# Eleven identity products during the first load, and the rests of the first group's odd heads moved together, in a decoder layer on one core

## The chip, the cores and the metric

The kernel runs on one core of a Trainium2 chip. A core has five engines that run beside each other and meet at semaphores: TensorE (PE in the profile; its weight loads are shown as PEld), VectorE (DVE), ScalarE (ACT), GpSimd (POOL) and SyncE (SP), which here only issues transfers. ACT and POOL issue a few transfers too. All transfers run on the core's 16 DMA engines. The metric is the device time of one execution in microseconds (us), the median of several.

## What is computed

One decoder layer over 16 sequences of 128 tokens with 256 channels, all in float32. It has three residual steps; only the first matters here, latent attention with 16 heads of 72 latent channels:

```python
h = layernorm(x)                                        # 16 x 128 x 256
Wdkv = h @ latent_w + latent_b                          # keys and values, 72 wide
q = einsum('btc,hcl->bhtl', h, Wd_w) + Wd_b[None, :, None, :]
scores = einsum('bhtl,bsl->bhts', q, Wdkv) / sqrt(16)   # then causal mask
y = einsum('bhts,bsl->bhtl', softmax(scores), Wdkv)
x = x + y.transpose(0, 2, 1, 3).reshape(b, t, 16 * 72) @ out_w + out_b
```

The second step mixes a context tensor in by a decaying sum that runs in both directions over the tokens (a WKV step). The third is a mixture of 8 experts of which each token uses two: tokens are sorted into lists by expert, and the experts' products run over slots of 128 listed tokens.

## The kernel before

**Stages.** Sequences are handled two at a time, a group (GB = 2, eight groups). A unit is one sequence with one set of four heads (HG = 4), so there are 64 units. A loop at the end of the program runs over steps: step s makes the scores, maxima and exponentials of unit s, normalizes unit s - 1, and turns the probabilities and makes the values of unit s - 2. The work of the next group, of the WKV step and of the routing is spread over the same steps by a written plan (`at(step, place, function)`; the places of a step are called "pre", A, B, C and D). After 64 steps come the expert slots. Each engine carries out its instructions in exactly the order in which the program writes them.

**The start.** Before the loop comes group 0's preparation, in this order: `masks()` makes two constants on POOL, identb (a 128 x 128 identity in bf16) and maskb (the causal mask of four heads, 128 x 512 in bf16). `group_stats(0)` and `group_norm(0)` normalize the first two sequences, `group_turn(0)` turns them on PE (L349) and `group_turned(0)` copies the result, xnT, out of PSUM on DVE (L353). `group_latents(0)` makes keys and values (L363), and `query_tile` (L404) with `query_tile_out` (L410, on ACT) makes and evicts query tiles 0 to 3. A float32 product shows in the trace as two instructions of half its work each, called halves below.

**Query tiles and rests.** Queries are made channels by tokens. Two heads of 72 channels would need 144 rows, but a tile has 128. So each of eight tiles (NP = 8) holds an even head's 72 channels and 56 of the odd head's (LB = 56); the 16 channels left over from each odd head (LR = 16) are made together in a ninth tile, `qrest`, the tile of the rests. Its weights `wqr_sb` are gathered by a POOL copy (L1206). Tiles 0 to 3 form the even set q0 (q[0, 0]), tiles 4 to 7 the even set q2 (q[0, 2]).

The odd sets q1 and q3 hold odd heads with all 72 channels in order. `odd_queries(g, u)` puts set 2u + 1 together by transfers from SBUF to SBUF: one copy of 56 partitions with 4 KB each from the even set (L422), and the 16 remaining rows. For group 0 the rests come from `qrest` by four transfers of 16 KB, one for each head (L425); later groups take another way by DRAM (L428).

**Order around the change.** `first_rest`, planned for step 0 at "pre", stands just behind the scores of unit 0. It makes and evicts the tile of rests, puts q1 together, and starts `load_outw()`: three transfers of 1152 KB in all, the weights of the output projection (L191 to L193), that are needed in step 5. Tiles 4 and 5 come in step 0, tiles 6 and 7 in step 1, and `odd_queries(0, 1)` puts q3 together in step 1 as soon as tile 7 is evicted. The scores of unit 1 (L440, L442) need q1, those of unit 2 need q2, those of unit 3 need q3. All these transfers are issued by SP, one after another; an issue that waits keeps all later ones back. ACT makes the exponentials of unit 1 ahead of the evictions of tiles 6 and 7.

**Pools.** `bank("mm", ...)` hands out PSUM banks from a pair in turn; latents and query tiles use it. Sets of queries live in `qpool`, with five buffers for tag "q", handed out in the order in which the program asks.

The functions that the change touches, with the lines that the profile names:

Of the kernel before, what the change touches and what calls it, by code (L numbers as in the profile page):

```python
# [9 lines left out]
F32 = mybir.dt.float32  # L10
# [8 lines left out]
P = 128  # L19
# [6 lines left out]
L = 72  # L26
# [5 lines left out]
GT = GB * T  # L32
HG = 4
# [3 lines left out]
NP = H // 2  # L37
LB = P - L
# [41 lines left out]
def decoder_kernel(  # L80
# [19 lines left out]
    nc = tc.nc  # L100
# [14 lines left out]
    qpool = st.enter_context(tc.tile_pool(name="qpool", bufs=5))  # L115
# [12 lines left out]
    def bank(tag, name, bufs=2):  # L128
        return psum.tile([P, 512], F32, tag=tag, name=name, bufs=bufs)
# [59 lines left out]
    def load_outw():  # L189
        outw2 = outw.rearrange("l (i o) c -> l i o c", o=2)  # L190
        nc.sync.dma_start(outw_sb[0:L, 0:NP, :], outw2[:, :, 0, :])  # L191
        nc.sync.dma_start(outw_sb[L:P, 0:NP, :], outw2[0:LB, :, 1, :])
        nc.sync.dma_start(  # L193
            outw_sb[:, NP, :], outw[LB:L].rearrange("r (i o) c -> (r i) o c", o=2)[:, 1, :]
        )
# [19 lines left out]
    identb = wpool.tile([P, P], BF16, tag="identb", name="identb")  # L215
    maskb = wpool.tile([P, HG, T], BF16, tag="maskb", name="maskb")
# [3 lines left out]
    def masks():  # L220
        nc.gpsimd.tensor_copy(identb, ident)
        nc.gpsimd.memset(maskb, 0.0)
        nc.gpsimd.affine_select(
            out=maskb,
            in_=maskb,
            compare_op=ALU.is_ge,
            fill=NEG,
            base=0,
            pattern=[[0, HG], [-1, T]],
            channel_multiplier=1,  # L230
        )
# [64 lines left out]
    def rstd_of(var, n, name):  # L296

        nc.vector.tensor_scalar_add(var, var, EPS)
        rs = small.tile([P, GB], F32, tag="rs", name=f"rs_{name}")
        nc.gpsimd.tensor_tensor(rs[:, :n], var, mhalf[:, :n], ALU.pow)  # L300
        return rs

    def stats(mv, src, name):
        bn = small.tile([P, 6], F32, tag="bn", name=f"bn_{name}")
        nc.vector.bn_stats(bn, src)
        nc.vector.bn_aggr(mv, bn)


    mva, rsa, xns, pxns, xnT, kvT, kvN, q, qrest = {}, {}, {}, {}, {}, {}, {}, {}, {}

    def group_stats(g):
        mva[g] = small.tile([P, GB, 2], F32, tag="mv4", name=f"mv4_{g}", bufs=2)
        for i in range(GB):
            stats(mva[g][:, i, :], xs[g * GB + i], f"a{g}_{i}")
        rsa[g] = rstd_of(mva[g][:, :, 1], GB, f"a{g}")
# [7 lines left out]
    def group_norm(g):  # L323
        mv, rs = mva.pop(g), rsa.pop(g)
        xns[g] = []
        nb = less_mean(mv[:, :, 0], rs, GB, f"a{g}") if g else None
        for i in range(GB):
            xt = xs[g * GB + i]
            xn = wk.tile([P, C], F32, tag="xn", name=f"xn_{g}_{i}")
            if g:  # L330
                nc.scalar.activation(
                    xn, xt, AF.Identity, bias=nb[:, i : i + 1], scale=rs[:, i : i + 1]
                )
            else:
                nc.vector.tensor_scalar(
                    xn, xt, mv[:, i, 0:1], rs[:, i : i + 1], ALU.subtract, ALU.mult
                )
            xns[g].append(xn)
# [51 lines left out]
    def query_tile(g, i):  # L390

        u, j = divmod(i, HG)
        if i == NP:
            qrest[g] = qpool.tile([P, GT], F32, tag="qr", name=f"qr_{g}", bufs=1)
            to = qrest[g]
            w = wqr_sb.rearrange("p c r i -> p c (r i)")
        else:
            if j == 0:
                q[g, 2 * u] = qpool.tile([P, HG, GT], F32, tag="q", name=f"q_{g}_{2 * u}")
            to = q[g, 2 * u][:, j, :]  # L400
            w = wq_sb[:, :, i, 0:P]
        pq = bank("mm", f"pq_{g}_{i}")
        for c in range(NC):
            nc.tensor.matmul(  # L404
                pq[:, :GT], w[:, c, :], xnT[g][:, c, :], start=(c == 0), stop=(c == NC - 1)
            )
        return pq, to

    def query_tile_out(g, i, pq, to):
        nc.scalar.activation(to, pq[:, :GT], AF.Identity, bias=bq_sb[:, i : i + 1], scale=0.25)  # L410
# [7 lines left out]

    def odd_queries(g, u):

        qb = qpool.tile([L, HG, GT], F32, tag="q", name=f"q_{g}_{2 * u + 1}")
        nc.sync.dma_start(qb[0:LB], q[g, 2 * u][L:P])  # L422
        if g == 0:
            for j in range(HG):
                nc.sync.dma_start(qb[LB:L, j, :], qrest[g][u * HG + j : P : NP, :])  # L425
        else:
            qd = qds[g].rearrange("(r i) t -> r i t", i=NP)
            nc.sync.dma_start(qb[LB:L], qd[:, ts(u, HG), :])  # L428
        q[g, 2 * u + 1] = qb


    pss, probs, sums_of, pts, aTs, pys, yP, yds, pos = {}, {}, {}, {}, {}, {}, {}, {}, {}
# [758 lines left out]


    masks()
    group_stats(0)
    group_norm(0)
    group_turn(0)
# [12 lines left out]

    def first_rest():  # L1210
        query_tile_out(0, NP, *query_tile(0, NP))
        odd_queries(0, 0)
        load_outw()

    at(0, "pre", first_rest)

    late_tiles = {0: [4, 5], 1: [6, 7]}
# [12 lines left out]
    for s in range(SLOT0 + len(ORDER) + 1):  # L1230
        j = s - SLOT0
# [22 lines left out]
        g, i = divmod(s, UG)  # L1254
# [12 lines left out]
        for n, t in tiles:  # L1267
            if t == NP:
                rest_queries(n)
            if t == 5 and n:  # L1270
                odd_queries(n, 0)
            if t == 7:
                odd_queries(n, 1)
# [68 lines left out]
```

## Time and profile before

| | |
|---|---|
| Three timed runs | 552.07, 553.12 and 553.45 us, median 553.12 |
| The profiled execution | 554.7 us; its span, from first to last instruction, 553.0 |
| Mean granted TensorE clock | 0.984 |
| First tokens' statistics on DVE begin | 3.68 us (they waited for the transfer of x) |
| First turn of group 0 on PE | 6.54 us |
| Scores of unit 0, unit 1, unit 2, unit 3 begin on PE | 15.64, 20.02, 24.37, 31.10 us |
| PE waited longest in total for | DVE xn (L349), 6.5 us, once, at the start |

The profile's times are microseconds from the start of the span. The timeline lists an engine's instructions in order; neighbours of one kind are merged and counted (x8 is eight of them). A PE line's length includes the modelled end of a pipelined product, so the pace is better read from the distance between starts. "Idle before <- releaser" gives how long the engine did nothing and what ended it. SPq and ACTq lines are issues of transfers: their length is that of the issue, not of the transfer. The windows view adds up each engine's busy time in a stretch, with the clock that TensorE was granted (1.00 is full) and the busy share of the DMA engines.

### The profile page before, as it was taken

Reading aid. Unit: us, or ns where it says so; the run is one execution under the profiler, and the core shown is the slowest. Engines: PE = TensorE matmul, PEld = TensorE weight load, DVE = VectorE, ACT = ScalarE, POOL = GpSimd, SP = SyncE. Lnnn points to the kernel's source line nnn. Section 1 sums busy time; section 2 is a strip of 40 time slices with the busy share of each in tenths; the row PEclk is TensorE's granted clock in tenths of the full one; section 3 lists DMA queues with packets and bytes.
Section 4 is the critical chain, followed back from the end, with each engine's and each line's share of the span. In section 5 each row is a group of like instructions: output and inputs, shape, how many; then the busy total and the mean of one; then the engine's idle time right before and its main releaser. Section 6 shows DMA issues by size and latency. Waiting matters only on the chain. (4 is left out here: it accounts for less than half of the span.)

```text
span 553.0 us, 10138 instructions
## 1 busy us (share of the span) xinstructions
PE 512.8 (93%) x3272; PEld 439.2 (79%) x3272; DVE 330.6 (60%) x831; ACT 329.3 (60%) x953; POOL 327.1 (59%) x379
## 2 busy tenths in 40 slices
PE   4889999999999999999998989999989999989990
PEld 3768787887777887877875679989979999989980
DVE  3354776687887678888769776555644533333330
ACT  1788998898797888888986873434313232313200
POOL 5356647564787774697646976454875454541532
PEclk9999999999999999999998999999989999999996
DMA  5432245364365545131121113232234232325321
GB/s 149 98 88 67 70 133 170 121 198 120 110 182 133 170 130 178 41 98 37 52 79 56 40 53 66 38 65 45 40 40 51 48 51 47 51 47 173 58 30 19
DMA packets 39662, 47.59 MB, mean 86 GB/s; under 512 B 14136, under 2 KB 31416, under 8 KB 39576
## 3 DMA queue, kind: packets, MB, share of 16 engines
q1 hardware_dynamic: 30106, 37.20, 23.0%
q0 software_dynamic: 7936, 9.51, 11.2%
q8 instruction: 28, 0.46, 0.3%
q10 hardware_dynamic: 1566, 0.21, 0.3%
q14 instruction: 26, 0.21, 0.2%
HBM read 28.22 MB, written 13.31 MB: 75 GB/s over the span
## 5 line engine op out<-in xcount | busy, mean ns | idle before, releaser
L467 ACT ACTIVATE pr<-s,nm 128x128 f32<-128x128 f32 x256 | 90.7, 370 | 9.7 <-DVE nm L459 9.5
L480 POOL TENSOR_TENSOR pr<-pr,rsum 128x512 f32<-128x512 f32 x64 | 75.7, 1183 | 33.5 <-DVE rsum L479 25.6
L990 ACT ACTIVATE sl<-s 128x512 f32<-128x512 f32 x36 | 21.5, 598 | 120.7 <-PE s L980 104.9
L1018 POOL DMA_INDIRECT acc<-y,en x28 | 47.5, 1697 | 60.4 <-DVE y L1013 29.8
L442 PEld LDWEIGHTS s<-kvT,q 72*128 72x128 f32 x512 | 65.7, 191 | 18.7 <-issue 12.6
L980 PEld LDWEIGHTS s<-xT,w 128*128 128x128 f32 x576 | 70.5, 195 | 9.4 <-issue 6.7
L980 PE MATMUL s<-xT,w 128*128 128x128 f32 x576 | 72.0, 279 | 5.4 <-DVE xT L944 2.3
L520 PE MATMUL po<-outw_sb,yP 128*128 128x256 f32 x288 | 74.4, 385 | 0.6 <-DMA yP<-yd 0.6
L442 PE MATMUL s<-kvT,q 72*128 72x128 f32 x512 | 70.5, 279 | 3.2 <-DMA q<-qr 2.2
L980 PE MATMUL pu<-xT,w 128*128 128x128 f32 x576 | 70.5, 276 | 0.0
L992 DVE TENSOR_TENSOR hT<-sl,pu 128x512 f32<-128x512 f32 x36 | 24.7, 687 | 74.1 <-PE pu L980 56.9
L1002 PE MATMUL pd<-wall,hT 128*128 x288 | 68.0, 379 | 0.0
L494 PE MATMUL py<-aT,kvN 128*72 128x512 f32 x128 | 66.4, 600 | 1.6 <-ACT aT L488 1.3
L980 PEld LDWEIGHTS pu<-xT,w 128*128 128x128 f32 x576 | 67.7, 193 | 0.0
L404 PE MATMUL pq<-xnT,wq_sb 128*128 128x256 f32 x256 | 65.3, 387 | 0.0
L520 PEld LDWEIGHTS po<-outw_sb,yP 128*128 128x128 f32 x288 | 54.0, 193 | 13.1 <-issue 5.2
L459 DVE TENSOR_REDUCE nm<-s 128x4 f32<-128x512 f32 x64 | 43.6, 682 | 30.5 <-PE s L442 30.5
L1002 PEld LDWEIGHTS pd<-wall,hT 128*128 128x128 f32 x288 | 52.0, 190 | 5.6
L467 ACT ACTIVATION_READ_ACCUMULATOR pr<-s,nm 128x1 f32 x256 | 53.0, 207 | 0.0
L488 ACT COPY aT<-pt 128x512 f32<-128x512 f32 x64 | 37.2, 581 | 26.0 <-PE pt L486 24.6
L404 PEld LDWEIGHTS pq<-xnT,wq_sb 128*128 128x128 f32 x256 | 46.2, 195 | 5.0 <-issue 0.2
L912 POOL DMA_INDIRECT xr<-xn,en x36 | 37.4, 1040 | 13.3 <-issue 7.6
(172 smaller groups left out, 877.8 us busy)
## 6 DMA issues: line engine op xcount, KB each, us to landing
wall<-in_wg_dram SPq DMA_DIRECT2D x8, 512.0 KB
wall<-in_wu_dram SPq DMA_DIRECT2D x8, 512.0 KB
wall<-in_wd_dram SPq DMA_DIRECT2D x8, 512.0 KB
q<-q SPq DMA_DIRECT2D x16, 224.0 KB
yP<-yB SPq DMA_DIRECT2D x32, 112.0 KB
cx<-in_cx_dram SPq DMA_DIRECT2D x16, 128.0 KB
acc<-x SPq DMA_DIRECT2D x16, 128.0 KB
xn<-row SPq DMA_DIRECT2D x16, 128.0 KB
```

Source lines behind the costliest of these rows:

```text
L404: nc.tensor.matmul(pq[:, :GT], w[:, c, :], xnT[g][:, c, :], start=(c == 0), stop=(c == NC - 1))
L442: nc.tensor.matmul(ps[:, j, :], q[g, hg][0:L, j, ts(i, T)], kvT[g][:, ts(i, T)], start=False, stop=(j == HG - 1), skip_group_check=n >= 2,)
L459: nc.vector.tensor_reduce(nm, ps, AX.X, ALU.max, negate=True)
L467: nc.scalar.activation(pr[:, j, :], ps[:, j, :], AF.Exp, bias=nm[:, j : j + 1], accum_out=sums[:, j : j + 1],)
L480: nc.gpsimd.tensor_mul(pr, pr, rsum.unsqueeze(2).to_broadcast([P, HG, T]))
L488: nc.scalar.copy(aT, pt)
L494: nc.tensor.matmul(py[:L], kvN[g][:, ts(i, L)], aTs.pop((b, hg)), start=True, stop=True)
L520: nc.tensor.matmul(pos[b][:, :C], yP[b][:, i, :], outw_sb[:, i, :], start=(i == 0), stop=(i == NP))
L912: nc.gpsimd.indirect_dma_start(out=xr, out_offset=None, in_=xn2[0 : t["rows"], :], in_offset=bass.IndirectOffsetOnAxis(ap=entries[j][:, 0: ...
L980: nc.tensor.matmul(o[:, ts(f, P)], w[:, c * F + f * P : c * F + (f + 1) * P], xT[:, c, :], start=(c == 0), stop=(c == NC - 1),)
L1002: nc.tensor.matmul(pd[:, :C], hT[:, f, :], wall[:, bass.ds(e, 1), WD0 + f * C : WD0 + (f + 1) * C], start=(f == 0), stop=(f == NF - 1),)
L1018: nc.gpsimd.indirect_dma_start(out=acc if j < SF + S2 else out2, out_offset=bass.IndirectOffsetOnAxis(ap=en[:, 1:2], axis=0), in_=y, in_of ...
```

## The change

Two things are changed. Behind `masks()`, eleven products of identb and maskb are written to a PSUM bank from the pair "mm" that nothing reads. And the rests of both odd sets are moved by a new function, `first_odd(u)`, that asks for the odd set's buffer and issues its four transfers from `qrest`. `first_rest` calls it for q1 ahead of `odd_queries(0, 0)`, and for q3 behind it; `odd_queries` of group 0 now only issues the copy of 56 partitions.

```diff
     def odd_queries(g, u):
 
-        qb = qpool.tile([L, HG, GT], F32, tag="q", name=f"q_{g}_{2 * u + 1}")
-        nc.sync.dma_start(qb[0:LB], q[g, 2 * u][L:P])
         if g == 0:
-            for j in range(HG):
-                nc.sync.dma_start(qb[LB:L, j, :], qrest[g][u * HG + j : P : NP, :])
+            qb = q[g, 2 * u + 1]
+            nc.sync.dma_start(qb[0:LB], q[g, 2 * u][L:P])
         else:
+            qb = qpool.tile([L, HG, GT], F32, tag="q", name=f"q_{g}_{2 * u + 1}")
+            nc.sync.dma_start(qb[0:LB], q[g, 2 * u][L:P])
             qd = qds[g].rearrange("(r i) t -> r i t", i=NP)
             nc.sync.dma_start(qb[LB:L], qd[:, ts(u, HG), :])
         q[g, 2 * u + 1] = qb
+
+    def first_odd(u):
+
+        q[0, 2 * u + 1] = qpool.tile([L, HG, GT], F32, tag="q", name=f"q_0_{2 * u + 1}")
+        for j in range(HG):
+            nc.sync.dma_start(q[0, 2 * u + 1][LB:L, j, :], qrest[0][u * HG + j : P : NP, :])
...
     masks()
+
+    idle = bank("mm", "idle")
+    for _ in range(11):
+        nc.tensor.matmul(idle, identb, maskb, start=True, stop=True)
     group_stats(0)
...
     def first_rest():
         query_tile_out(0, NP, *query_tile(0, NP))
+        first_odd(0)
         odd_queries(0, 0)
+        first_odd(1)
         load_outw()
```

On SP the order of issues from the tile of rests on becomes: before, copy q0 to q1, four rests of q1, three of outw, copy q2 to q3, four rests of q3; after, four rests of q1, copy q0 to q1, four rests of q3, three of outw, copy q2 to q3. The buffer of q3 is now asked for ahead of q2's. The products have line 1203 in the changed kernel, the rests line 435, the copies of group 0 line 423.

## The prediction

> **What bounds the kernel now.** I read the page first, its busy shares and slices, to see which engine carries the span.
>
> ```profile
> PE 512.8 (93%) x3272; PEld 439.2 (79%) x3272; DVE 330.6 (60%) x831; ACT 329.3 (60%) x953; POOL 327.1 (59%) x379
> ...
> PE   4889999999999999999998989999989999989990
> ```
>
> TensorE is the bound, except in the first three slices (13.8 us each), and the change lies wholly in those. So I read the timeline there.
>
> ```profile
> 2.29 0.64 POOL L223 TENSOR_SCALAR_AFFINE_SELECT maskb<-maskb 128x512 bf16<-128x512 bf16 x1
> ...
> 6.54 1.11 PE L349 MATMUL pxn<-ident,xn 128*128 128x128 f32 x4 [6.54 <-DVE xn L335]
> ...
> 8.44 1.98 PE L363 MATMUL pk<-xnT,latw_sb 128*72 128x256 f32 x4 [0.79 <-DVE xnT L353]
> ...
> 13.77 0.47 ACT L410 ACTIVATE q<-pq,bq_sb 128x256 f32<-128x256 f32 x1 [1.12 <-PE pq L404]
> 14.63 0.47 ACT L410 ACTIVATE q<-pq,bq_sb 128x256 f32<-128x256 f32 x1 [0.39 <-PE pq L404]
> ...
> 15.99 0.94 SPq L422 DMA_DIRECT2D q<-q  x1
> ...
> 17.60 0.47 ACT L410 ACTIVATE qr<-pq,bq_sb 128x256 f32<-128x256 f32 x1 [1.63 <-PE pq L404]
> ...
> 18.10 2.49 SPq L425 DMA_DIRECT2D q<-qr  x4
> ...
> 19.12 0.38 PE L440 MATMUL s<-maskb,identb 128*128 128x512 bf16 x1
> ...
> 19.99 0.30 PEld L442 LDWEIGHTS s<-kvT,q 72*128 72x128 f32 x2 [0.98 <-DMA q<-q]
> ...
> 20.63 0.91 SPq L191 DMA_DIRECT2D outw_sb<-in_outw_dram  x1
> 20.65 0.30 PEld L442 LDWEIGHTS s<-kvT,q 72*128 72x128 f32 x2 [0.36 <-DMA q<-qr]
> ...
> 22.20 1.89 PE L404 MATMUL pq<-xnT,wq_sb 128*128 128x256 f32 x8
> ...
> 26.05 0.82 SPq L422 DMA_DIRECT2D q<-q  x1
> ...
> 26.92 2.56 SPq L425 DMA_DIRECT2D q<-qr  x4
> ...
> 31.07 0.97 PEld L442 LDWEIGHTS s<-kvT,q 72*128 72x128 f32 x8 [2.35 <-DMA q<-q]
> ```
>
> Each line gives start, length, engine, source line and operation, out<-in, how often, and in brackets the idle time before it and what ended it. The reader is to see three waits: for the first tokens (to 6.54), for the first odd set (19.99 to 21.9, one head at a time) and for the second odd set (to 31.07). From there nothing is loose; the windows say so, and show what pauses do to the clock. Columns are the stretch, its length, then each engine's busy time, granted clock and DMA share.
>
> ```profile
> 8.44:13.20 4.76, 4.76 (x11) 3.50 (x12) 1.07 (x3) 0.68 (x2) 3.72 (x14) 1.00 0.24 57
> ...
> 402.60:406.01 3.41, 1.27 (x8) 0.84 (x7) 1.87 (x4) 0.00 (x0) 2.97 (x5) 1.00 0.30 37
> 406.01:409.42 3.41, 3.41 (x19) 3.41 (x18) 1.44 (x7) 0.00 (x0) 2.97 (x3) 0.50 0.20 44
> 494.76:498.17 3.41, 1.60 (x10) 1.18 (x9) 0.83 (x3) 0.96 (x1) 1.58 (x1) 1.00 0.16 45
> ```
>
> PE between 32 and 80 us is busy 48.00 of 48.00 in the same view, so what the third scores' DMA costs at 32 us arrives at the end undiminished.
>
> **The eleven products.** They need maskb, ready at 2.29 + 0.64 = 2.93, so they start at about 3.0, on a PE idle to 6.54. Their price is the pace. One half of an f32 product over 256 columns costs 4.76/11 = 0.43 us before 13.2 (the granted clock column reads 1.00 and does not tell), and (19.12 - 17.39)/8 = 0.216 later, with the eight halves that begin at 17.39. The same halving stands between the evictions, 1.60 apart (12.17 to 13.77) and then 0.86. A bf16 product over 512 columns was followed by its successor 0.22 later (15.42 to 15.64) at the fast pace; at the slow one I take twice that, 0.43. Its weight load (0.10, the same view) runs beside the product before it. So eleven end between 3.0 + 2.4 = 5.4 and 3.0 + 4.7 = 7.7. I take 7.7: the trace shows slow pace through 4.76 us of unbroken work, as long as these eleven. The first turn is then late by 7.7 - 6.54 = 1.15, hidden up to 6.54 by the load.
>
> What they can buy: from 8.44 to 15.29 twenty halves run (four of pk, sixteen of pq), 6.85 us; at 0.215 they take 4.3. Gain 2.55, net 1.4. Call T the end of the rest tile's eviction: 17.60 + 0.47 = 18.07 before, 16.67 after. Bounds: 15.5 (no lateness), 19.2 (late, and no fast pace earned). Covers hold: the rest tile's weights are copied by POOL at 12.55 to 13.16 and needed at 15.1; the extra bank taken from the pair "mm" has no reader.
>
> The Trainium skill ("TensorE: Matmul & The Clock Gate", Part 1, on the HAM clock gate) says that the clock doubles after a busy window of some 3.4 us, that these windows run freely, and that an idle window halves it again. By that rule alone T could be anything between the two bounds from one execution to the next. The rows agree with the size (3.41 us at 0.50 from 406.01), and the trace's record of the granted clock changes at 13.48, 296.79, 406.02 and 542.55, all whole multiples of 3.413 apart.
>
> **The rests, moved.** Before, SP issued: copy q0 to q1 at 15.99 (L422), four rests at 18.10 (0.62 each), outw at 20.63. After: four rests of q1 at T, then the copy q0 to q1 (0.94), then four rests of q3, then outw. The copy does not depend on the rest tile, yet now queues on SP behind four issues that wait for it. It was issued 2.11 before the rests; now it is issued T + 0.03 + 2.49 = T + 2.52. Its landing: issued at 15.99, its packets stop by 19.2 in the windows of DMA traffic, so 3.2 us (bounds: 1.9 for the small rests, 18.10 to 20.0; 4.75 for its like at 26.05 behind outw). It lands at T + 5.7 and then all four heads run. Before, the scores ended at 22.20 = T + 4.13. After: T + 5.7 + 0.1 + 8 x 0.11 = T + 6.7 (0.11 is a half over 128 columns: eight fill 15.64 to 16.53). Loss 2.55, against a gain of 1.4: 23.4 instead of 22.20. Behind this wait on PE stand two query tiles, the turn of group 1 and the third scores; ACT's exponentials wait for it.
>
> The skill ("DMA: Bandwidth & Descriptors", Latency and other measured facts) gives a fixed cost of about 2 us. With 2 in place of 3.2 the loss would be 1.35; but the row has the same transfer at 3.2, and it decides.
>
> **The pause.** PE has nothing from T + 1.3 (19.12 + 0.22 before) to T + 5.8, 4.5 us. A stretch of 3.41 with 1.27 busy (402.60) was followed by one at 0.50; one with 1.60 (494.76) was not. Any such grid puts at least half of 4.5 idle in one stretch, so at most 1.16 busy: slow again. Price 3.41/2 = 1.7 to twice that. Cover: the next wait. PE's work from these scores to the end of the first value product (29.43) is 24 halves at 0.11 (two sets of scores, two turns), 16 at 0.215 (pk and three query tiles) and two at 0.43, about 7.0 us; 22.5 + 7.0 + 1.7 = 31.2, or 32.9 for twice, against the third wait's end below, 32.8. At nothing, then; up to 1.7 if that cover is gone.
>
> **The second odd set.** Its rests no longer follow its copy, which buys little: the copy itself lands at about 30.8 (31.07 waits on q<-q). That copy, issued at 26.05, lies behind outw's 1.15 MB (576, 448 and 128 KB in the list of issues): the windows have DMA at 0.83 from 22.2 to 29.9. And outw moves from 20.63 to T + 0.03 + 2.49 + 0.94 + 2.49 = T + 5.95 = 22.62, later by 2.0. Nothing earlier needs the engines, so the copy lands at 32.8 (its own issue, some 27.5 at worst, plus 3.2 is earlier). Scores end at 32.8 + 0.1 + 0.9 = 33.75; before 31.10 + 8 halves = 32.06. Sum: +1.7. With T = 15.5, +0.5; with 19.2, +4.2. q3's buffer swaps with q2's in the pool of five, which costs nothing: group 1's users wait for PE's scores anyway.
>
> The profiled execution took 554.7 (span 553.0, 1.7 around it), 1.6 above the median of the three timed runs, 553.12. I put the difference on the median: 554.8.
>
> **Rivals.**
> 1. Products pay fully: fast pace before 7.2, T 15.5 to 16.1, +0.5 to +1.1: 553.6 to 554.2. For: no matmul competes to 6.54. Against: 4.76 us slow after 8.44.
> 2. Products do not do what they say: the copy of xnT (0.8 us idle) breaks the work, the pace stays slow, T 18 to 19.2, +3 to +4.2: 556.1 to 557.3. For: 2.6 us of work in 6.66 to 10.07 had not sufficed. Against: eleven in a row are longer.
> 3. Faster: the two half-speed stretches at 296.79 and 406.01 cost 1.7 each, after pauses of 1.7 and 2.3 us. If a shifted start puts both pauses astride two stretches, as at 494.76, 3.4 goes: 554.8 - 3.4 = 551.4. It decides only when both vanish.
>
> **Numbers.** A measurement of this kernel tells 0.3% (1.7 us) from no change: 551.46 and 554.78 are the borders. My case (554.3 to 555.5) 0.46, rival 1 0.26, rival 2 0.18, rival 3 0.10. Of my case about 0.32 lies over the border, so slower 0.50, same 0.40, faster 0.10. The likeliest's own range is 554.3 to 555.5; to hold 8 in 10 it reaches through rivals 1 and most of 2, with half a microsecond of scatter: 552.2 to 557.0.
>
> **What would show it.** Eleven L1203 products from 3.0; evictions of the first query tiles 0.86 apart from the first; scores of the first odd set starting all together at 22 to 23 after a pause of some 4.5 us that names q<-q; halves at 0.43 after it; outw at 22 or later; the third scores at 32 to 33. I am wrong if the copy to q1 lands within 2 us, if outw's delay doesn't reach the second copy, or if PE after 33 us makes up the loss.

## The result and the profile after

Fifteen timed runs of each kernel, side by side, gave 555.86 us median for the changed kernel (553.22 to 557.83) and 552.36 for the kernel before (550.71 to 553.6). The ratio is 1.0054, 95% interval 1.0039 to 1.0070: the change costs 3.0 us, between 2.2 and 3.9. In a second measurement (e8 below) the changed kernel had 1.0040 (1.0019 to 1.0062), 2.2 us. The kernel before had medians from 552 to 557 us on the chips of this study, so below only ratios are compared; they are turned into microseconds with 555. Two executions of the kernel before, of 901 and 1084 us, are left out of every comparison.

The profiled execution of the changed kernel took 554.74 us, its span 553.0, the same span as that of the kernel before. The two profiles thus do not show the loss in their ends, but they show it clearly at the start. Timeline of the changed kernel, lines of TensorE, ACT and SP, with columns as before:

```profile
2.98 3.91 PE L1203 MATMUL idle<-maskb,identb 128*128 128x512 bf16 x11 [2.98 <-POOL maskb L223]
6.73 0.60 PE L349 MATMUL pxn<-ident,xn 128*128 128x128 f32 x4
8.11 1.08 PE L363 MATMUL pk<-xnT,latw_sb 128*72 128x256 f32 x4 [0.78 <-DVE xnT L353]
...
15.07 0.47 ACT L410 ACTIVATE qr<-pq,bq_sb 128x256 f32<-128x256 f32 x1 [1.91 <-PE pq L404]
...
15.57 2.49 SPq L435 DMA_DIRECT2D q<-qr  x4
...
18.11 0.91 SPq L423 DMA_DIRECT2D q<-q  x1
...
19.07 2.44 SPq L435 DMA_DIRECT2D q<-qr  x4
...
21.47 2.05 PE L448 MATMUL s<-kvT,q 72*128 72x128 f32 x8 [4.70 <-DMA q<-q]
21.55 0.90 SPq L191 DMA_DIRECT2D outw_sb<-in_outw_dram  x1
...
27.21 0.82 SPq L423 DMA_DIRECT2D q<-q  x1
...
32.63 1.16 PE L448 MATMUL s<-kvT,q 72*128 72x128 f32 x8 [1.60 <-DMA q<-q]
```

The eleven products run from 2.98 to 6.73, and the four halves of pk take 1.08 us where they took 1.98. The tile of rests is evicted at 15.07 + 0.47 = 15.54, 2.5 us earlier than before. By the scores of unit 1 that lead is gone: they begin at 21.47 after a pause that ended with the copy q0 to q1, where they began at 20.02. The scores of unit 3 begin at 32.63 instead of 31.10, and again it is a copy (q2 to q3) that ends the wait. The 1.5 us stay: the scores of unit 7 begin at 49.51 against 47.96.

The windows of the same profile show the clock (columns: stretch, length, busy time of PE, PEld, DVE, ACT, POOL with instructions, granted clock, DMA share, GB/s):

```profile
19.46:22.87 3.41, 1.40 (x6) 1.44 (x7) 0.00 (x0) 0.00 (x0) 0.32 (x1) 0.50 0.31 87
22.87:26.28 3.41, 3.41 (x11) 2.80 (x10) 0.69 (x1) 1.97 (x9) 0.00 (x0) 0.50 0.71 184
26.28:29.69 3.41, 3.41 (x25) 3.02 (x24) 1.81 (x4) 3.00 (x12) 2.12 (x3) 1.00 0.99 200
...
33.62:80.00 46.38, 46.38 (x269) 37.47 (x268) 27.05 (x59) 41.32 (x142) 26.19 (x27) 1.00 0.27 74
```

After the pause TensorE works at half pace for two stretches, and from the third scores on it is busy without a gap, as before. That the spans end equal has its reason later. The record of the granted clock has in both profiles a stretch of 3.41 us at 0.50 near 297 (from 296.79 before, from 299.35 now), and in the profile of before a second one (from 406.02) that this one has not. The changed kernel is still 1.8 us behind at the first product of the expert slots (tile pd, 334.7 against 332.9), and 0.6 ahead at the last one (536.9 against 537.5). So 2.4 us were made up where that second stretch lies, and 0.6 of them go again behind the last product. By its length I estimate the stretch at 3.41/2 = 1.7 us; the rest I can't place. Two more profiles of the changed kernel have neither stretch.

### The profile page after: what moved, and what is told of

It reads as the page before. It is cut to its first block, busy times and chain, and to the rows that moved or that the text cites. A ratio compares the mean times of both kernels' runs of the same rounds, so it can differ in the third digit from the quotient of the medians.

```text
span 553.0 us, 10159 instructions
## 1 busy us (share of the span) xinstructions
PE 513.4 (93%) x3282; PEld 438.5 (79%) x3283; DVE 330.0 (60%) x831; ACT 329.0 (59%) x953; POOL 327.3 (59%) x379
## 5 line engine op out<-in xcount | busy, mean ns | idle before, releaser
L986 PEld LDWEIGHTS s<-xT,w 128*128 128x128 f32 x576 | 69.3, 192 | 8.1 <-issue 5.4
L986 PE MATMUL s<-xT,w 128*128 128x128 f32 x576 | 70.7, 276 | 4.1 <-DVE xT L950 2.2
L465 DVE TENSOR_REDUCE nm<-s 128x4 f32<-128x512 f32 x64 | 43.6, 682 | 32.6 <-PE s L448 32.5
```

Source lines behind the costliest of these rows:

```text
L465: nc.vector.tensor_reduce(nm, ps, AX.X, ALU.max, negate=True)
L986: nc.tensor.matmul(o[:, ts(f, P)], w[:, c * F + f * P : c * F + (f + 1) * P], xT[:, c, :], start=(c == 0), stop=(c == NC - 1),)
```

## The experiments

Theory A at the outset was the recorded one: the order of issues on SP loses, the products win. The rivals were that the products do not pay (B), and that the scatter or the fall of the clock is the loss (C). The numbers below are read off the timelines: T, the end of the eviction of rests; the first issue of outw; the issue of the copy q2 to q3; the start of the third scores (unit 3); and the start of the scores of unit 7, by which the start is over. "Slow stretch" below is a stretch at a granted clock of 0.50.

| kernel | T | outw | copy q2 to q3 | third scores | unit 7 (against before) | ratio to before |
|---|---|---|---|---|---|---|
| before | 18.07 | 20.63 | 26.05 | 31.10 | 47.96 | 1 |
| changed, three profiles | 15.3 to 15.9 | 21.3 to 21.9 | 27.1 to 27.8 | 32.3 to 32.6 | 49.2 to 49.5 (+1.2 to +1.6) | 1.0054, 1.0040 |
| e1 products alone | 16.36 | 18.91 | 24.33 | 30.21 | 48.68 (+0.7) | 0.9978 |
| e2 move alone | 17.28 | 23.28 | 29.18 | 34.02 | 50.92 (+3.0) | 1.0069 |
| e3 copy first | 15.89 | 20.97 | 23.87 | 32.37 | 51.80 (+3.8) | 1.0056 |
| e5 pause filled | 15.80 | 21.82 | 26.53 | 32.69 | 51.20 (+3.2) | 1.0062 |
| e6 outw last | 16.55 | 29.31 | 28.47 | 33.62 | 50.52 (+2.6) | 1.0033 |
| e10 e6, pause filled | 15.96 | 27.53 | 26.69 | 30.07 | 46.85 (-1.1) | 0.9946 |
| e7 before, outw last | 17.89 | 29.21 | 25.86 | 29.23 | 47.77 (-0.2) | 1.0011 |
| e9 order alone | 17.83 | 26.66 | 25.83 | 29.20 | 46.05 (-1.9) | 0.9950 |
| e4, e12 all three | 16.64, 15.85 | 25.45, 24.66 | 24.61, 23.82 | 27.98, 27.75 | 44.80, 44.65 (-3.2, -3.3) | 0.9919, 0.9938 |

The column of unit 7 is one profiled execution each, the ratio the median of several. They agree broadly, but not in size: e1 and e10 took 1.9 us less than their starts say, and the changed kernel about a microsecond more.

**The two parts alone.** e1 is the kernel before with the products:

```diff
     masks()
+    idle = bank("mm", "idle")
+    for _ in range(11):
+        nc.tensor.matmul(idle, identb, maskb, start=True, stop=True)
```

> The eleven products alone, transfers ordered as before. Theory A (the order of issues on SP loses, the products win): the tile of rests is evicted 1.4 to 2.5 us earlier than at 18.07, everything behind it moves along, the outw transfers too (issued near 18.5 to 19.2), so the third wait ends 1.4 to 2.5 us earlier than 31.07 and the time falls by 1.0 to 2.5 us (about 0.3%). Rival B (the products do not pay, they only delay the first turn): no change to +1.2 us. Rival C (scatter of the clock's slow stretches in the middle of the run decides): any sign, without the start being earlier.

Measured: 0.9978 (0.9958 to 0.9998), 1.2 us less, so B's range is missed, though narrowly. The start of the profiled execution does not show the gain:

```profile
30.21 1.13 PE L442 MATMUL s<-kvT,q 72*128 72x128 f32 x8 [2.34 <-DMA q<-qr]
34.98 1.27 PE L442 MATMUL s<-kvT,q 72*128 72x128 f32 x8
```

```profile
28.50:31.91 3.41, 1.70 (x14) 1.71 (x15) 0.53 (x1) 0.46 (x2) 3.27 (x4) 1.00 0.42 126
31.91:35.32 3.41, 3.41 (x10) 1.82 (x9) 0.43 (x3) 2.82 (x11) 1.04 (x1) 0.50 0.01 2
```

The lead of 1.7 at T is 0.9 at the third scores, whose wait there is long enough that the clock falls once behind it; from the third to the fourth scores pass 4.77 us instead of 3.28, and at unit 7 the kernel is 0.7 behind. That profiled execution (556.03) is one of six with a mean granted clock of 0.981 or less, which took 556.03 to 558.29; the other six, at 0.983 or more, took 553.75 to 555.75. Whether those lack the slow stretch at 31.91 or a later one is not on record, so the products' gain alone is measured but its place is not shown.

e2 is the changed kernel without those products.

> The moved rests alone, no products. Theory A: rests evicted at 18.1 as before, the copy q0 to q1 issued at 20.6 and landed at 23.8, scores of unit 1 end near 24.7 instead of 22.2, outw issued at 24.0, the third scores begin near 34.5, the time is 3 to 4.5 us over the kernel before. Rival B (it was the products that lost): no change within 0.5 us.

Measured: 1.0069 (1.0046 to 1.0092), 3.8 us more. So the whole loss sits in the moved rests, as theory A had it. The start shows that the products give back a part: +3.0 at unit 7 without them, +1.2 to +1.6 with them.

**Which wait is it?** e3 takes away the late first copy and leaves outw late:

```diff
     def first_odd(u):
         q[0, 2 * u + 1] = qpool.tile(...)
+        if u == 0:
+            nc.sync.dma_start(q[0, 1][0:LB], q[0, 0][L:P])
         for j in range(HG):
```

(The copy is then not issued a second time in `odd_queries`.)

> The changed kernel with the copy q0 to q1 issued ahead of its four rests again; q3's rests stay early. Theory A: the first pause shrinks to what it was before, scores of unit 1 end 1.4 to 2.5 us earlier than 22.2; but q3's rests still hold back outw by 2.5 us, so the second copy lands 0 to 1 us later than before and the time is within 1 us of the kernel before, 2 to 3.5 us under the changed one. If the delay of the first copy were not what costs, it would stay 3 us above before.

Measured: 1.0056 (1.0033 to 1.0079). A miss: 3.1 us more than before, no better than the changed kernel. Timeline and windows of e3:

```profile
23.87 0.82 SPq L424 DMA_DIRECT2D q<-q  x1
...
26.91 1.02 PE L503 MATMUL py<-aT,kvN 128*72 128x512 f32 x2
32.37 2.08 PE L451 MATMUL s<-kvT,q 72*128 72x128 f32 x8 [4.44 <-DMA q<-q]
```

```profile
27.53:30.94 3.41, 0.40 (x1) 0.00 (x0) 0.40 (x2) 1.39 (x3) 2.93 (x4) 1.00 1.01 192
30.94:34.35 3.41, 1.98 (x9) 1.98 (x10) 0.00 (x0) 0.00 (x0) 0.51 (x1) 0.50 0.21 59
34.35:37.77 3.42, 3.42 (x11) 2.36 (x10) 0.87 (x2) 2.40 (x10) 0.09 (x1) 0.50 0.01 2
```

The first wait has shrunk to what it was, and the second copy is issued 3.3 us earlier than in the changed kernel; but the third scores begin within 0.3 us of it. The copy lies behind outw, with DMA at 1.01 of its time. What was won goes into one longer pause of 4.4 us, and the fall of the clock that follows lies where TensorE has no other wait to hide it: from the third to the fourth scores (32.37 to 38.27) pass 5.90 us instead of 3.28. From here theory A2: the place of outw sets the third wait, and a pause costs its fall of the clock only where nothing covers it. Over the eight profiles in which outw goes ahead of the second copy, the third scores begin 10.5 to 11.4 us after outw's first issue, although the copy itself is issued anywhere from 2.9 to 5.9 us after it.

e4 is e3 with `load_outw()` moved from `first_rest` to behind `odd_queries(0, 1)` in step 1:

```diff
         odd_queries(0, 0)
         first_odd(1)
-        load_outw()
...
             if t == 7:
                 odd_queries(n, 1)
+                if n == 0:
+                    load_outw()
```

> As e3, and the three outw transfers issued behind the copy q2 to q3 instead of ahead of it (needed first in step 5). Theory A with the queue behind outw as the second half of the loss: the second copy, issued near 24.5, lands 3.2 us later, near 27.7, the third scores begin near 28 as soon as PE is there, and the time falls by 2.5 to 4 us under the kernel before (about 549). If the second copy's landing were not due to outw, it would be like e3.

Measured: 0.9919 (0.9891 to 0.9948), 4.5 us less; 3.2 of them are there at unit 7. There is no wait for a transfer at the third scores any more; TensorE comes straight from the first values:

```profile
27.12 1.02 PE L503 MATMUL py<-aT,kvN 128*72 128x512 f32 x2
27.98 1.07 PE L451 MATMUL s<-kvT,q 72*128 72x128 f32 x8
```

**Is the fall of the clock the loss?** e5 is the changed kernel with 20 more products behind the mask of unit 1, into a bank that nothing reads:

```diff
             nc.tensor.matmul(ps, identb, maskb, start=True, stop=False)
+        if n == 1:
+            fill = bank("o", "fill", bufs=1)
+            for _ in range(20):
+                nc.tensor.matmul(fill, identb, maskb, start=True, stop=True)
```

> The changed kernel with 20 further identity products (into a PSUM bank that nothing reads) between the mask and the scores of unit 1, so that PE works through the first pause. Theory A2 (the third wait, set by the place of outw in the queue, is the loss; what comes before it is covered): no slow stretch of the clock from 19 to 26, scores of unit 1 end about 1 us earlier, the third scores begin at 32 to 33 all the same, and the time is 2 to 4.5 us over the kernel before, as the changed kernel was (3.0). Rival C2 (the fall of the clock in the first pause is the loss): 1.5 to 3 us less than the changed kernel, so 0 to 1.5 over the kernel before.

Measured: 1.0062 (1.0040 to 1.0085), 3.4 us more than before; C2 falls for the changed kernel. The second copy is issued 0.7 us earlier and the third scores begin at 32.69 all the same. The fall of the clock has only changed its place; the fourth scores begin 4.97 us behind the third, 1.7 more than before:

```profile
32.69 1.16 PE L452 MATMUL s<-kvT,q 72*128 72x128 f32 x8 [2.62 <-DMA q<-q]
37.66 1.10 PE L452 MATMUL s<-kvT,q 72*128 72x128 f32 x8
```

```profile
30.80:34.21 3.41, 1.52 (x13) 1.52 (x14) 0.32 (x1) 0.26 (x1) 3.17 (x4) 1.00 0.36 89
34.21:37.62 3.41, 3.41 (x9) 1.71 (x8) 0.55 (x2) 2.58 (x10) 0.95 (x1) 0.50 0.01 2
```

**outw alone.** e6 is the changed kernel with e4's edit and nothing else; its first copy is as late as in the change.

> The changed kernel with one edit: the three outw transfers are issued behind the copy q2 to q3. The copy q0 to q1 is as late as in the change. Theory A2: the second copy lands 3.2 us after its issue at about 27, the third scores begin near 31 as soon as PE gets there, and the time is 1 us under to 0.5 over the kernel before, 2.5 to 4 under the changed one. If the late first copy is what costs (my recorded step), 1.5 to 3 over the kernel before remain.

Measured: 1.0033 (1.0015 to 1.0050), 1.8 us more: a miss for A2, a hit for the other line, my recorded step. With outw out of the way the late first copy decides. Windows of e6, then of e10, which adds e5's 20 products:

```profile
18.65:22.07 3.42, 0.00 (x0) 0.00 (x0) 0.00 (x0) 1.72 (x4) 2.13 (x3) 1.00 0.31 86
22.07:25.48 3.41, 3.01 (x11) 2.86 (x12) 0.69 (x1) 0.20 (x1) 0.00 (x0) 0.50 0.04 10
25.48:28.89 3.41, 3.41 (x12) 2.77 (x12) 0.07 (x1) 3.22 (x13) 0.07 (x1) 0.50 0.00 0
```

```profile
18.65:22.07 3.42, 3.25 (x17) 1.40 (x15) 0.00 (x0) 1.12 (x3) 1.54 (x3) 1.00 0.31 86
22.07:25.48 3.41, 3.41 (x24) 3.10 (x23) 0.96 (x2) 1.68 (x9) 0.00 (x0) 1.00 0.04 10
```

> e6 (outw behind the second copy, first copy still late) with the 20 filling products of e5 in the first pause. If it is the fall of the clock in that pause that makes the late first copy cost once outw is out of the way: query tiles 6 and 7 run at the full pace, the second copy is issued near 26.5 instead of 28.5, the third scores begin near 30, and the time is 2 to 3 us under e6 (ratio to before 0.997 to 1.000). If it is the late copy itself, less than 1 us under e6 (1.002 or more).

Measured: 0.9946 (0.9924 to 0.9967), 3.0 us less than before and 4.8 less than e6. TensorE does 24 instructions instead of 11 in the stretch from 22.07. So in this setting the fall of the clock is most of what e6 loses. Of the 3.55 us between the third scores (33.62 and 30.07), 0.6 is T, and 0.8 is a wait of e6 for its second copy (told below); some 2.1 are left for the clock. The late copy by itself is not free either: e10's third scores begin 2.1 to 2.3 us behind those of e4 and e12, where that copy goes first.

The timed runs lie 4.8 us apart, more than the 3.7 of the starts, and e10's gain is more than was expected. The mean granted clock differs too: nine of e10's twelve executions had 0.989 or more, none of e6's twelve had more than 0.984. In e10's profile there is no slow stretch before 539, in e6's there are three between 298 and 415. Why the middle of the run differs is open.

**The kernel before, with outw last.** e7 makes e4's edit to the kernel before.

> The kernel before with that same edit and nothing else. Theory A2: the third wait is then set by q3's rests, whose last issue near 28.9 lands near 30.7; the third scores end about 1 us earlier than before, the time falls by 0.5 to 1.5 us. If the place of outw were of no account in the kernel before, no change within 0.3 us.

Measured: 1.0011 (0.9995 to 1.0027): no change that can be told, against an expected gain of 0.5 to 1.5 us. The third scores do begin at 29.23, 1.9 earlier, but they take 0.5 longer, and the rest of the gain is gone at the first projection:

```profile
41.16 1.13 PE L520 MATMUL po<-outw_sb,yP 128*128 128x256 f32 x4 [0.87 <-DMA yP<-yB]
```

Only 0.2 is left at unit 7. The projection waits for a transfer issued at 34.52 behind outw, which in e7 is issued only at 29.21, behind q3's four late rests. With these rests moved early as well, that is e9 (e4 without the products), outw goes out at 26.66 and the projection begins at 39.55.

> e4 without the eleven products: the copy q0 to q1 first, then all eight rests, then the copy q2 to q3, then outw. Theory A2: the third scores begin near 29.5 as soon as PE gets there, 1.5 us earlier than before, and outw, issued near 27, is in time for its first use; the time falls by 1 to 2 us. So of e4's 4.5 us the products hold 2 to 3, more than the 1.2 they gave alone, where the wait for outw's queue came behind them. If the products' share is the same 1.2 in both places, this one lies 3 us or more under the kernel before.

Measured: 0.9950 (0.9929 to 0.9970), 2.8 us less, of which 1.9 are there at unit 7. The rest lies in the middle, as in e10: nine of the ten executions had a mean granted clock of 0.990 or more, and none of the nineteen of the kernel before beside them had more than 0.988. So the early rests of q3, one half of the change, are worth having once the copy q0 to q1 and the copy q2 to q3 go ahead of what they used to go ahead of.

Three runs are repeats: e8 and e11 of the changed kernel, e12 of e4.

> The changed kernel once more, on the chip of the other runs: 2 to 4 us over the kernel before (3.0 measured). Its profile shows which of the numbers of the start change from one execution to the next: by theory A2 the order of issues and the third scores near T + 17.1 (T the eviction of the rests), T itself between 15.3 and 19.

> The changed kernel a third time, one look, for the scatter of T and of the clock: T between 15.3 and 19, third scores near T + 17.1, slow stretch of the clock in the first pause again.

> e4 once more (products, copy q0 to q1 first, eight rests, copy q2 to q3, then outw): ratio to the kernel before 0.989 to 0.995 as in its first run; its third scores begin near 28 without a wait for a transfer, and there is no slow stretch of the clock before 290. If the products are worth nothing beside the order (e9 had 0.995), the ratio is 0.994 to 0.997.

Measured: e8 1.0040; e11, a single execution, T 15.28, third scores 32.28, the slow stretch from 19.48 again; e12 0.9938 (0.9909 to 0.9967). In all three profiles of the changed kernel T is 15.3 to 15.9 and the third scores lie 16.7 to 17.1 us behind it, and unit 7 is 1.2 to 1.6 us later than before. So the scatter (C) does not make the loss of the start. e12's profile has one slow stretch from 20.64 that was not expected. The share of the products in e4 is not settled: e4 and e12 lie 0.7 to 1.7 us under e9, with intervals that overlap; at unit 7 they are 1.3 to 1.4 ahead of it.

## Why the prediction was right, and where it was off

The direction and the mechanism held; the size was only roughly right. The forecast of 554.8 us was 1.1 under the measured 555.86, which lies in the stated range but above that of the likeliest case (554.3 to 555.5). The forecast difference of 1.7 us stands against a measured 3.0 (2.2 to 3.9), or 2.2 in the second measurement.

- **The products.** Start 3.0 forecast, 2.98 found. I took all eleven as slow and so the first turn as 1.15 late; the fast pace came while they ran (the trace has starts 0.43 apart up to 5.49 and 0.22 from 5.86), and the turn was 0.19 late, at 6.73. T came out as 15.54, at the lower bound of 15.5, instead of 16.67. This term was mis-sized by 1.1 us, in favour of the change.
- **The first copy.** Forecast T + 2.52 for its issue and T + 5.8 for the scores; found 18.11 = T + 2.57 and 21.47 = T + 5.93. The copy landed at 21.33, 3.2 us after its issue: the row of before was the right size. The fixed cost of about 2 us that the Trainium skill states ("DMA: Bandwidth & Descriptors", Latency and other measured facts) is not enough for this copy taken alone.
- **The pause.** Forecast 4.5 us and a fall of the clock that costs 1.7 to 3.4, covered by the third wait. Found 4.70 idle, two slow stretches, and cover enough: TensorE still waited 1.60 for the third scores. e5 shows the cover (filling the pause gains nothing). The price without cover shows from the third to the fourth scores: 1.5 (e1) and 1.7 (e5) for one slow stretch, 2.6 for the two of e3; between e6 and e10 it is some 2.1.
- **outw and the second copy.** Its issue at T + 5.95 was found at 21.55 = T + 6.0. I took the copy to land 10.2 after outw's first issue, by the one profile of before; it landed at 32.58, 11.0 after. This term was 0.8 short and made up most of what T had gained: third scores ended with +1.6 us, forecast +1.7. That these agree so well is luck: two terms were off in opposite directions, and for T = 15.5 alone the recorded text had +0.5.
- **The end.** The 1.6 us are in the timeline from 33 us on, and still there at unit 7. The other 0.6 to 1.4 us of the measured loss no profile shows; the three profiled executions of the changed kernel, 554.74, 554.35 and 555.27 us, lie under the medians 555.86 and 555.78. The longer executions go with a lower mean granted clock: of the fifteen timed ones, the five at 0.980 or more took 553.22 to 554.74 us, the ten below it 555.58 to 557.83. In the second measurement the five at 0.984 or more took 554.33 to 555.33, the six below 555.78 to 559.2. Where their further slow stretches lie, and whether the change brings them about, stays open.
- **Rivals.** Rival 1 had T right (15.5 to 16.1) and the rest too small. Rival 2 did not come up in any of the ten profiles with products at the start: T never passed 16.7. Of rival 3 one part happened: the profile of the change lacks one of the two slow stretches, those of e8 and e11 lack both. These executions took 554.35 and 555.27 us, where the kernel before had medians of 554.1 and 555.2: about level with it, not 1.7 under it.

That of two waits the later decides was in the recorded text: it put the first at nothing as long as the third scores' wait covers it. What it did not say is that then removing one of them alone gains little. Taking away the first alone (e3) gives 1.0056, taking away the second alone (e6) 1.0033, both (e4) 0.9919. The expectation of e3 had the third scores nearly right (0 to 1 us later than before, found 1.3); what it left out is the longer pause in front of them, whose fall of the clock took the 2.6 us behind them.

## What to carry to other kernels

When a transfer is moved ahead in a queue, list what stood behind it and when each is needed: eight rests move only 16 KB each, but each holds the queue for 0.62 us, and together they held back a copy that had been ready, and 1.15 MB that in turn lay ahead of the next copy. Weights that are needed some twenty microseconds later (outw is issued at 21.55 and first used at 43.01) belong behind the small copies that the next step waits for, though not so far behind that they become the next wait (e7). And if removing one wait changes nothing, look for the second before giving the first up; a pause moved is a fall of the clock moved, to where it may be covered by nothing.

## What was unexpected of the hardware

The clock's stretches of 3.413 us do not part cleanly by TensorE's busy time. In the fourteen profiles every stretch at the full clock with at most 1.52 of 3.41 busy was followed by a slow one. Between 1.60 and 2.45 both happen: 1.70 (e1, from 28.50) and 2.44 (e3, from 17.29) were followed by a slow stretch, 1.60 (kernel before, 494.76) and 2.45 (kernel before, 27.14) were not. A slow stretch of partial work (1.98 busy, e3 from 30.94; 3.01, e6 from 22.07) was followed by another slow one; those that were followed by the full clock were busy throughout. What is counted besides time these runs don't tell.

In e6 all reports of the second copy's parts but one had come by 31.6, the last at 33.58. On the DMA engines an instruction fetch of 16 KB, from 29.58 and for 1.43 us, falls into this time:

```profile
q1 hardware_dynamic: 70, 0.23, 52.2%
q8 instruction: 1, 0.02, 5.6%
```

(Queues with packets, MB and share of sixteen engines, e6 from 29.5 to 31.1.) It may have held back the late part, but its 1.43 us are less than the 2.0 that the last report is late, and it was not tried separately.
